# Cross-attention and FFN on one core: when the rows of later groups are normalized and turned, and which engine forms the weight sums of the first group

## Chip, core and metric

The kernel runs on one core of a Trainium2 chip. The metric is the device time of one execution in microseconds. In the profile PE is TensorE (PEld its weight loads), DVE is VectorE, ACT is ScalarE, POOL is GpSimd and SP is SyncE, which issues nearly all the DMAs.

## What is computed

Sixteen sequences of 128 tokens with 1024 features go through one block: cross-attention on a context of the same shape, and a linear layer with fixed 0/1 weights. All is float32.

```python
x = x + xattn(layernorm(x), ctx, ctx, Wq, bq, Wk, bk, Wv, bv, Wo, bo)   # 32 query heads, 8 key heads of 32
x = x + scale * (concat(n[:819], -4 * n[819:]) @ kernel)                # n = layernorm(x), kernel 1024x1024 of 0/1
```

Wq and Wo are 1024x1024, Wk and Wv 1024x256. In attention each key head serves four query heads; the softmax runs over 128 keys.

## The kernel before, in words

**Groups and stages.** The 16 sequences (batches b) are worked in eight groups of two. Each group passes: context transposed, keys (`prep_k`) and values (`prep_v`); x normalized and transposed, queries (`prep_q`); four *attends*, one for each batch and each half a of the heads, in the order (b0, a0), (b1, a0), (b0, a1), (b1, a1); the output product (`out_proj`); the second norm and the FFN (`ffn`). The stages of neighbouring groups overlap: while group g's four attends run, PE also does the output product of g-1, keys, values and queries of g+1 and the FFN of g-1. In the first group that filler is the rest of its own queries and the keys, values and queries of group 1.

**Order of the work.** The order on each engine is written out by the program: `Stream` holds a queue of generators that emit pieces of PE work with a planned duration, and events put in with `later(us, fn)` that are emitted when the planned clock has passed. Planned times only choose the order; on the chip each engine works through its own queue in order and waits for semaphores. So an instruction that waits holds up all that stands behind it on its engine.

**An attend.** `scores` (L559) makes four score tiles; for each, DVE takes the maximum (negm, L571), ACT four exponentials (L575), DVE a reciprocal and a product (inv, p, L586 and L587), PE turns p (tpp, L592), ACT copies it (pt, L594); `weighted` (L602) multiplies with the values.

**Products by seven.** Queries of group 1 on and all output products use a seven-product scheme for 2x2 blocks (`seven`, L453). It needs sums of weight blocks: `combine` (L767) forms them once, in the first group, on DVE (L781: four steps of two 128x512 operations each for Wq's halves k = 0 and 1 and for Wo's halves 0 and 1), and SP stores them to DRAM (L784). Weight pieces of 512 KB are read into a ring of eight buffers (`fetch`, L219), each when PE has used up an earlier one. The queries of the first group alone are made plainly (`prep_q_plain`, L413, eight outputs; ACT writes batch 0's and DVE batch 1's, L430 and L433).

**Norms and transposes.** `norm_x` (L381) normalizes rows in place: two statistics, an aggregate and an addition on DVE, the reciprocal root on GpSimd (L285), the scaling on DVE (L286). The rows of groups 0 and 1 are then transposed by PE (`turned`, L334). From group 2 on, `turn_x` (L348) normalizes, has SP store the rows to DRAM and load them back by 32-row blocks (`through_dram`, L296), and DVE turns the blocks (L361). The context is turned by DVE (`turn_ctx`, L343). Rows x, blocks turn_x and turn_f share two buffers of the tag "turn".

**Where the change touches.** `get_x` (L859) loads x of a group and plans its `turn_x`; both are called, with `prep_ctx`, at the start of the group before the one they serve, beside the output product (L916, L917). In the first group L898 to L913 give the order; `sums_of_wo` (L847) and `sums_of_wq` (L875) spread the weight sums. `load_by_quadrants` (L160) loads Wk and Wv in four DMAs each, `through_dram` of the second norm is timed by `FBACK` (L814) and `late` (L683).

Of the kernel before, what the change touches and what calls it, by code (L numbers as in the profile page):

```python
# [17 lines left out]
P = 128  # L18
# [58 lines left out]
def once(fn, *args):  # L77
    fn(*args)
    yield 0.0
# [3 lines left out]
def kernel(  # L83
# [74 lines left out]
        cs[b] = c_t  # L158

    def load_by_quadrants(dst, w, queues):  # L160
        src = w.rearrange("(k c f) n -> k f c n", k=NB, f=32)
        for k in range(NB):
            queues[k % len(queues)].dma_start(out=dst[k * 32 : (k + 1) * 32], in_=src[k])

    def load_x(b, tag="row"):

# [178 lines left out]
            src[:, :, h * HC : (h + 1) * HC],  # L345
        )

    def turn_x(b, store, back, turn):  # L348

        grp, j = b // GB, b % GB  # L350
        src = xns.pop(b)
        stats = new_stats(f"a{b}")
        for k in range(D // HALF):
            half_stats(stats, src, k)
        row = work.tile([P, D], FP, tag="row", name=f"xq{b}", bufs=2)
        normalize(by_quadrant(row), by_chunk(src), stats, f"a{b}")

        def blocks(c_t, h=0):
            if (grp, h) not in xTs:
                xTs[grp, h] = work.tile([P, HC, T], FP, tag="tT", name=f"xT{grp}_{h}", bufs=TB)  # L360
            nc.vector.transpose(  # L361
                xTs[grp, h][:, :, j * S : (j + 1) * S].rearrange("p c (t n) -> p t c n", t=NB),
                c_t[:, :, h * HC : (h + 1) * HC],
            )
            if h == 0:
                stream.later(1.5, lambda: blocks(c_t, 1))

        through_dram(row, f"x{b}", store, back, turn, blocks)

    def prep_ctx(grp, *us):  # L370

        for n, at in enumerate(us):
            stream.later(at, lambda n=n: turn_ctx(grp * GB + n % GB, n // GB))

    def prep_x(grp, h):
# [37 lines left out]
    def prep_q_plain(a, at):  # L413

        for j in range(GB):
            qTs[j, a] = work.tile(S4, FP, tag="qT", name=f"qT{j}_{a}", bufs=6)
        for g in range(NG):
            mm = ps_mm.tile([P, GB, S], FP, tag="mm", name=f"q_{a}_{g}")
            k, cols = g // 2, slice(g % 2 * P, (g % 2 + 1) * P)
            yield from accumulate(  # L420
                mm,
                [
                    (
                        pieces[at[c // HC, k]].rearrange("p (c n) -> p c n", c=HC)[:, c % HC, cols],
                        chunk(xTs, 0, c),
                    )
                    for c in range(NC)
                ],
            )
            nc.scalar.activation(  # L430
                qTs[0, a][:, g], mm[:, 0], AF.Identity, bias=bqs[:, a, g : g + 1], scale=scale
            )
            nc.vector.tensor_scalar(  # L433
                qTs[1, a][:, g], mm[:, 1], scale, bqs[:, a, g : g + 1], MULT, ADD
            )
            yield 0.85

    def product(mm, pairs, start):
# [175 lines left out]
    def out_proj(grp):  # L614
# [12 lines left out]
        def run():  # L627
            b0 = grp * GB
            half = {f"a{j + 1}{a + 1}": yTs.pop((b0 + j, a)) for j in range(GB) for a in range(NA)}
            s = {n: work.tile(S4, FP, tag="comb", name=f"s{n}_{grp}", bufs=4) for n in range(1, 5)}  # L630

            def sum_(n, left, right, op):
                left = s[left] if left in s else half[left]
                right = s[right] if right in s else half[right]
                nc.vector.tensor_tensor(s[n], left, right, op)
# [12 lines left out]
            def product_of(prod, mm, start):  # L648
                lhsT = half[prod.split()[0]]
                for k in range(2):  # L650
                    w = pieces[ids[prod, k]].rearrange("p (c n) -> p c n", c=2)
                    for c in range(2):
                        nc.tensor.matmul(  # L653
                            mm,
                            lhsT=lhsT[:, 2 * k + c],
                            rhs=w[:, c],
                            start=start and k == c == 0,
                            stop=k == c == 1,
                            skip_group_check=True,
                        )  # L660
                    fetch()
                    yield 2 * HALF / 600

            def read(mm, c):
                j, h = int(c[1]) - 1, int(c[2]) - 1
                x_t, cols = xs[b0 + j], slice(h * HALF, (h + 1) * HALF)
                nc.vector.tensor_add(x_t[:, cols], mm, x_t[:, cols])  # L667
                reads[c] += 1
                if reads[c] < (1 if c == "c21" else 2):
                    return  # L670
                stream.later(1.0, lambda: half_stats(stats[j], x_t, h) and None)
                if c in ("c12", "c21"):
                    def norm():
                        b = b0 + j
                        x2n = work.tile([P, D], FP, tag="row", name=f"x2n{b}", bufs=2)
                        if b < B - 2 * GB:
                            normalize(by_quadrant(x2n), by_chunk(x_t), stats[j], f"f{b}")
                            through_dram(x2n, f"f{b}", 3.0, *FBACK[j], lambda t: split_blocks(b, t))
                        else:
                            normalize(x2n, x_t, stats[j], f"f{b}")  # L680
                            x2ns[b] = x2n

                    late = 0.0 if b0 + j >= B - 2 * GB else 4.0  # L683
                    stream.later(late + (3.0 if c == "c12" else 4.5), norm)

            yield from seven(f"o{grp}", product_of, read)
# [77 lines left out]
            stream.later(0.7 + 2.4 * i, first)  # L764
        return pts

    def combine(w, k, part):  # L767

        if w == "q":

# [7 lines left out]
        for dst, left, right, op in ops:  # L778
            for h in range(2):
                cols = slice(h * HALF, (h + 1) * HALF)  # L780
                nc.vector.tensor_tensor(dst[:, cols], left[:, cols], right[:, cols], op)  # L781
            yield
        for n, t in enumerate(order):
            nc.sync.dma_start(out=sums[w, n + 1, k], in_=t)  # L784
# [16 lines left out]
    def load_o_part(k):  # L801
# [7 lines left out]
                part[r, o] = t  # L809
        return part  # L810

    BLOCKS = [(r, o) for r in range(2) for o in range(2)]
    NGRP = B // GB
    FBACK = ((12.0, 22.0), (14.0, 26.0))  # L814
    with tc.manual_schedule():
        stream = Stream()

# [27 lines left out]
            norm_x(j)  # L845

        def sums_of_wo():  # L847
            def then():
                o_parts.append(load_o_part(1))
                for j in range(GB):  # L850
                    load_x(GB + j, "turn")
                load_ffn()

            stream.later(4.0, lambda: spread(combine("o", 0, o_parts[0]), 1.5, then))

        stream.add(prep_x(0, 0), prep_x(0, 1), once(sums_of_wo), plain(0))
        stream.run(0.0, lambda: stream.queue)

        def get_x(grp):  # L859

            for j in range(GB):
# [29 lines left out]
        for grp in range(NGRP):  # L891
# [121 lines left out]
```

## Time and profile before

| | |
|---|---|
| median of 3 runs | 805.54 us (805.47 to 806.14) |
| the profiled execution | 805.76 us |
| its span, first to last instruction | 804.0 us |
| PE busy | 773.9 us (96%) |
| DVE busy | 489.1 us (61%) |
| ACT busy | 321.4 us (40%) |
| POOL busy | 71.0 us (9%) |
| mean granted PE clock | 0.996 |
| moved by DMA | 190.31 MB |

A row of a timeline gives start, length, engine, line, operation, what is written and read, and in brackets the idle time before it with the one who ended it. A row of waits gives engine and line, who was waited for, total us, times, and the longest. Matmuls of 128x128 weights start every 0.11, 0.22 or 0.43 us for 128, 256 or 512 columns when nothing holds them; the lengths shown are longer, since they overlap.

### The profile page before, as it was taken

The page shows a single profiled execution, that of the slowest core. Times are in us where ns is not written, and L with a number is a line of the kernel's source. Part 1 is how long each engine was busy: PE and PEld are TensorE (multiplying, and loading weights), DVE is VectorE, ACT ScalarE, POOL GpSimd, SP SyncE. Part 2 cuts the span into 40 slices and gives each one's busy share as a digit, 9 for nine tenths or more (in the row PEclk, how much of TensorE's full clock was granted, in tenths as well). Part 3 has the DMA queues.
Part 4 walks back from the last instruction along what each step waited for, and adds up shares of the span by engine and source line. Part 5 has one row for each costly group of instructions (what it writes and reads, how often), then busy time and mean ns, then how long its engine had stood idle before and what let it go on. Part 6 is the DMA issues. An engine that isn't in the chain of part 4 may idle for free.

```text
span 804.0 us, 13722 instructions
## 1 busy us (share of the span) xinstructions
PE 773.9 (96%) x5024; PEld 574.4 (71%) x5024; DVE 489.1 (61%) x910; ACT 321.4 (40%) x1257; POOL 71.0 (9%) x109
## 2 busy tenths in 40 slices
PE   3998999999999999999999999999999999999998
PEld 3886795589846897479864798548984689646556
DVE  1369756756487564866647575675647856567442
ACT  0143674344334352344433444334434445466100
POOL 1000003010010201001010100102001010100300
PEclk9999899999999999999999999999999999999999
DMA  9999499888488983889659984689847867562511
GB/s 204 360 312 319 155 372 393 265 252 270 143 283 271 249 263 140 305 252 283 208 188 293 271 264 156 244 263 261 263 158 270 293 198 260 181 214 74 197 45 79
DMA packets 98355, 190.31 MB, mean 237 GB/s; under 512 B 7888, under 2 KB 57040, under 8 KB 98288
## 3 DMA queue, kind: packets, MB, share of 16 engines
q1 hardware_dynamic: 96480, 187.73, 72.4%
q10 hardware_dynamic: 1664, 1.57, 1.1%
q8 instruction: 40, 0.66, 0.3%
q0 software_dynamic: 144, 0.14, 0.1%
q14 instruction: 27, 0.22, 0.1%
HBM read 160.04 MB, written 29.36 MB: 236 GB/s over the span
## 4 chain that ended last, share of the span: by engine, by line
PE 76%; DVE 12%; DMA 6%; issue 3%; SPq 1%; POOL 1%; ACT 0%; ACTq 0%; POOLq 0%; DVEq 0%
PE f L317 15%; PE q_u L442 13%; PE o_u L653 9%; PE q_v L442 6%; PE v L317 6%; PE tpp L592 6%; PE k L317 5%; PE o_v L653 5%; PE sc L559 4%; PE av L602 4%; PE q_c L442 3%; DVE p L587 2%; DVE st_a L277 2%; DVE x L667 2%; DVE cT L343 2%
## 5 line engine op out<-in xcount | busy, mean ns | idle before, releaser
L575 ACT ACTIVATE p<-sc,negm 128x128 f32<-128x128 f32 x512 | 181.0, 368 | 152.8 <-DVE negm L571 91.6
L594 ACT COPY pt<-tpp 128x512 f32<-128x512 f32 x128 | 74.6, 589 | 139.7 <-PE tpp L592 139.2
L571 DVE TENSOR_REDUCE negm<-sc 128x4 f32<-128x512 f32 x128 | 86.9, 681 | 38.2 <-PE sc L559 37.5
L317 PE MATMUL f<-wf_sb,x2l 128*128 128x512 f32 x256 | 105.4, 412 | 0.0
L575 ACT ACTIVATION_READ_ACCUMULATOR p<-sc,negm 128x1 f32 x512 | 105.2, 205 | 0.0
L317 PE MATMUL f<-wf_sb,x2h 128*128 128x512 f32 x256 | 101.1, 395 | 0.0
L587 DVE TENSOR_TENSOR p<-p,inv 128x512 f32<-128x512 f32 x128 | 89.8, 701 | 4.4
L179 POOL TENSOR_TENSOR x<-x,bo_b 128x256 f32<-128x256 f32 x64 | 50.2, 815 | 376.4 <-DMA x<-in_x_dram 318.5
L592 PE MATMUL tpp<-ident,p 128*128 128x128 f32 x512 | 76.8, 275 | 6.1 <-DVE p L587 4.0
L592 PEld LDWEIGHTS tpp<-ident,p 128*128 128x128 f32 x512 | 62.6, 142 | 27.6 <-issue 18.1
L442 PE MATMUL q_u<-t,piece 128*128 128x128 f32 x672 | 80.9, 275 | 0.0
L442 PEld LDWEIGHTS q_u<-t,piece 128*128 128x128 f32 x672 | 77.9, 192 | 0.0
L317 PE MATMUL v<-wv_sb,cT 128*128 128x256 f32 x256 | 63.0, 397 | 12.1 <-DMA wv_sb<-in_L_xattn_Wv_dram 12.1
L737 DVE SCALAR_TENSOR_TENSOR x<-f,fscale,x 128x512 f32<-128x512 f32 x32 | 24.0, 750 | 75.0 <-PE f L317 74.9
L653 PE MATMUL o_v<-piece,s 128*128 128x512 f32 x128 | 60.8, 601 | 2.9 <-DVE x L667 2.9
L653 PE MATMUL o_u<-piece,s 128*128 128x512 f32 x128 | 59.6, 598 | 3.4 <-DVE x L667 3.4
L317 PEld LDWEIGHTS v<-wv_sb,cT 128*128 128x128 f32 x256 | 49.6, 201 | 18.6 <-issue 12.1
L653 PE MATMUL o_u<-piece,yT 128*128 128x512 f32 x128 | 58.5, 599 | 0.0
L317 PE MATMUL k<-cT,wk_sb 128*128 128x256 f32 x256 | 57.8, 379 | 0.0
L317 PEld LDWEIGHTS f<-wf_sb,x2l 128*128 128x128 f32 x256 | 48.2, 188 | 10.9 <-issue 1.1
L317 PEld LDWEIGHTS f<-wf_sb,x2h 128*128 128x128 f32 x256 | 48.2, 188 | 10.3 <-issue 0.5
L317 PEld LDWEIGHTS k<-cT,wk_sb 128*128 128x128 f32 x256 | 48.0, 190 | 8.9 <-issue 2.6
(82 smaller groups left out, 911.9 us busy)
## 6 DMA issues: line engine op xcount, KB each, us to landing
piece<-o SPq DMA_DIRECT2D x64, 512.0 KB, 4.4
piece<-q SPq DMA_DIRECT2D x56, 512.0 KB, 5.9
piece<-in_L_xattn_Wq_dram SPq DMA_DIRECT2D x50, 512.0 KB, 5.8
piece<-in_L_xattn_Wo_dram SPq DMA_DIRECT2D x48, 512.0 KB, 4.5
xn<-in_x_dram SPq DMA_DIRECT2D x16, 512.0 KB, 5.4
x<-in_x_dram SPq DMA_DIRECT2D x16, 512.0 KB, 4.9
ctx<-in_ctx_dram SPq DMA_DIRECT2D x60, 128.0 KB, 7.3
out_dram<-x SPq DMA_DIRECT2D x15, 512.0 KB, 3.0
```

The source lines that it names most:

```text
L179: lambda cut=cut: nc.gpsimd.tensor_add(x_t[:, cut], x_t[:, cut], bo_b[:, cut]) and None,
L317: nc.tensor.matmul(mm, lhsT=lhsT, rhs=rhs, start=k == 0, stop=k == n - 1)
L442: nc.tensor.matmul(mm if part is None else mm[:, part], lhsT=lhsT, rhs=rhs, start=start and n == k == 0, stop=k == len(some) - 1, skip_gro ...
L559: nc.tensor.matmul(tiles[i][:, g], lhsT=qT[rows, g], rhs=kT[rows, a, cols], start=True, stop=True,)
L571: nc.vector.tensor_reduce(negm, tile_, AX.X, ALU.max, negate=True)
L575: nc.scalar.activation(p[:, g], tile_[:, g], AF.Exp, bias=negm[:, g : g + 1], accum_out=total[:, g : g + 1],)
L587: nc.vector.tensor_mul(p, p, inv.unsqueeze(2).to_broadcast([P, NG, S]))
L592: nc.tensor.transpose(tp[:, g], p[:, g], ident)
L594: nc.scalar.copy(pt, tp)
L602: nc.tensor.matmul(mm[i * HD : (i + 1) * HD], lhsT=vs[b][:, h * HD : (h + 1) * HD], rhs=pts[i], start=True, stop=True,)
L653: nc.tensor.matmul(mm, lhsT=lhsT[:, 2 * k + c], rhs=w[:, c], start=start and k == c == 0, stop=k == c == 1, skip_group_check=True,)
L737: nc.vector.scalar_tensor_tensor(x_t[:, cut], mm, fscale, x_t[:, cut], ALU.mult, ALU.add)
```

## The change

1. Rows of x for groups 2 to 7 are loaded, normalized and sent through DRAM (`get_x`, `rows_x`) one group earlier, beside the FFN (for group 2: beside the queries of group 1); the contexts are turned there too. The turning of the rows stays in the following group (`turn_rows`), at planned 30 to 36 us. The second norm is planned 4 us later, its way through DRAM shorter (`late`, `FBACK`).
2. `combine` takes an engine; Wo's sums and Wq's for k = 1 go to GpSimd, Wq's for k = 0 stay on DVE.
3. In the first group ACT writes the queries of both batches for a = 0.
4. Rows of group 1 are normalized inside the second plain product (after its 7th and 13th piece of work) and not after Wq's sums; they and the FFN weights are loaded before the second part of Wo, not after.
5. Wk and Wv are loaded in halves of four chunks: eight DMAs each, not four.

```diff
     def load_by_quadrants(dst, w, queues):
         src = w.rearrange("(k c f) n -> k f c n", k=NB, f=32)
-        for k in range(NB):
-            queues[k % len(queues)].dma_start(out=dst[k * 32 : (k + 1) * 32], in_=src[k])
+        for h in range(2):
+            cut = slice(h * NC // 2, (h + 1) * NC // 2)
+            for k in range(NB):
+                queues[k % len(queues)].dma_start(
+                    out=dst[k * 32 : (k + 1) * 32, cut], in_=src[k][:, cut]
+                )
...
-    def turn_x(b, store, back, turn):
-        grp, j = b // GB, b % GB
+    rows = {}
+    def rows_x(b):
         src = xns.pop(b)
...
         normalize(by_quadrant(row), by_chunk(src), stats, f"a{b}")
...
-            if h == 0:
-                stream.later(1.5, lambda: blocks(c_t, 1))
-        through_dram(row, f"x{b}", store, back, turn, blocks)
+        through_dram(row, f"x{b}", 2.5, 7.0, 7.0, lambda c_t: rows.update({b: c_t}))
+    def turn_x(b, h):
+        grp, j = b // GB, b % GB
...
+        c_t = rows.pop(b) if h == 1 else rows[b]
+        nc.vector.transpose(
+            xTs[grp, h][:, :, j * S : (j + 1) * S].rearrange("p c (t n) -> p t c n", t=NB),
+            c_t[:, :, h * HC : (h + 1) * HC],
+        )
...
-            nc.scalar.activation(
-                qTs[0, a][:, g], mm[:, 0], AF.Identity, bias=bqs[:, a, g : g + 1], scale=scale
-            )
-            nc.vector.tensor_scalar(
-                qTs[1, a][:, g], mm[:, 1], scale, bqs[:, a, g : g + 1], MULT, ADD
-            )
+            for j in range(GB):
+                if j == 0 or a == 0:
+                    nc.scalar.activation(
+                        qTs[j, a][:, g], mm[:, j], AF.Identity, bias=bqs[:, a, g : g + 1], scale=scale
+                    )
+                else:
+                    nc.vector.tensor_scalar(
+                        qTs[j, a][:, g], mm[:, j], scale, bqs[:, a, g : g + 1], MULT, ADD
+                    )
...
-                    late = 0.0 if b0 + j >= B - 2 * GB else 4.0
+                    late = 0.0 if b0 + j >= B - 2 * GB else 8.0
...
-    def combine(w, k, part):
+    def combine(w, k, part, engine=nc.gpsimd):
...
-                nc.vector.tensor_tensor(dst[:, cols], left[:, cols], right[:, cols], op)
+                engine.tensor_tensor(dst[:, cols], left[:, cols], right[:, cols], op)
...
-    FBACK = ((12.0, 22.0), (14.0, 26.0))
+    FBACK = ((7.0, 22.0), (8.0, 24.0))
...
         def sums_of_wo():
-            def then():
-                o_parts.append(load_o_part(1))
+            def inputs():
                 for j in range(GB):
                     load_x(GB + j, "turn")
                 load_ffn()
-            stream.later(4.0, lambda: spread(combine("o", 0, o_parts[0]), 1.5, then))
+            def then():
+                o_parts.append(load_o_part(1))
+            stream.later(10.0, inputs)
+            stream.later(8.0, lambda: spread(combine("o", 0, o_parts[0]), 3.3, then))
...
-                stream.later(10.0 + 3.0 * j, lambda b=b, j=j: turn_x(b, 3.5, 7.0 + j, 16.0 + 2.0 * j))
+                stream.later(5.0 + 4.0 * j, lambda b=b: rows_x(b))
+        def turn_rows(grp):
+            for n, at in enumerate((30.0, 32.0, 34.0, 36.0)):
+                stream.later(at, lambda n=n: turn_x(grp * GB + n // 2, n % 2))
...
-                    spread(combine("o", 1, o_parts[1]), 2.5)
-            spread(combine("q", k, {(r, o): pieces[at_q[r, o, k]] for r, o in BLOCKS}), 1.5, then)
+                    spread(combine("o", 1, o_parts[1]), 3.3)
+            part = {(r, o): pieces[at_q[r, o, k]] for r, o in BLOCKS}
+            if k == 0:
+                spread(combine("q", k, part, nc.vector), 1.5, then)
+            else:
+                spread(combine("q", k, part), 3.3, then)
...
                     once(prep_ctx, nxt, 12.5, 13.5),
-                    between(plain(1), 9, sums_of_wq, 0),
+                    between(
+                        between(between(plain(1), 7, norm_x, nxt * GB), 9, sums_of_wq, 0),
+                        13,
+                        norm_x,
+                        nxt * GB + 1,
+                    ),
                     once(sums_of_wq, 1),
                     once(turn_ctx, nxt * GB, 1),
                     once(turn_ctx, nxt * GB + 1, 1),
-                    once(norm_x, nxt * GB),
                     prep_k(nxt),
                     once(get_ctx, nxt + 1),
-                    once(norm_x, nxt * GB + 1),
                     prep_v(nxt),
                     prep_x(nxt, 0),
                     prep_x(nxt, 1),
+                    once(get_x, nxt + 1),
+                    once(prep_ctx, nxt + 1, 14.0, 18.0, 22.0, 26.0),
                     once(convert_ffn),
                     between(qs[nxt], 40, residuals, grp),
...
-                    once(get_x, nxt),
-                    once(prep_ctx, nxt, 3.7, 8.0, 13.0, 18.0),
+                    once(turn_rows, nxt),
                     os[grp - 1],
                     once(get_ctx, nxt + 1),
                     prep_k(nxt),
                     once(load_residual, b0, 4.0),
                     prep_v(nxt),
                     qs[nxt],
+                    once(get_x, nxt + 1),
+                    once(prep_ctx, nxt + 1, 2.5, 7.0, 11.0, 16.0),
                     ffn(p0),
                     once(load_residual, b1, 2.0),
```

More of the change, by code (lines that the diff above doesn't have):

```diff
@@ L356, in turn_x @@
         normalize(by_quadrant(row), by_chunk(src), stats, f"a{b}")
[L358 to L363, printed above, removed]
-            )
-            if h == 0:
-                stream.later(1.5, lambda: blocks(c_t, 1))
-        through_dram(row, f"x{b}", store, back, turn, blocks)
+        through_dram(row, f"x{b}", 2.5, 7.0, 7.0, lambda c_t: rows.update({b: c_t}))
+    def turn_x(b, h):
+        grp, j = b // GB, b % GB
+        if (grp, h) not in xTs:
+            xTs[grp, h] = work.tile([P, HC, T], FP, tag="tT", name=f"xT{grp}_{h}", bufs=TB)
+        c_t = rows.pop(b) if h == 1 else rows[b]
[3 more added lines that the diff above has]
+        )
     def prep_ctx(grp, *us):
-        for n, at in enumerate(us):
+        for n, at in enumerate(us if grp < NGRP else ()):
             stream.later(at, lambda n=n: turn_ctx(grp * GB + n % GB, n // GB))
@@ L429, in prep_q_plain @@
             )
-            nc.scalar.activation(
-                qTs[0, a][:, g], mm[:, 0], AF.Identity, bias=bqs[:, a, g : g + 1], scale=scale
-            )
-            nc.vector.tensor_scalar(
-                qTs[1, a][:, g], mm[:, 1], scale, bqs[:, a, g : g + 1], MULT, ADD
-            )
+            for j in range(GB):
[7 more added lines that the diff above has]
+                    )
             yield 0.85
@@ L810, in load_o_part @@
         return part
+    NGRP = B // GB
     BLOCKS = [(r, o) for r in range(2) for o in range(2)]
-    NGRP = B // GB
-    FBACK = ((12.0, 22.0), (14.0, 26.0))
+    FBACK = ((7.0, 22.0), (8.0, 24.0))
     with tc.manual_schedule():
@@ L859, in get_x @@
         def get_x(grp):
-            for j in range(GB):
+            for j in range(GB if grp < NGRP else 0):
                 b = grp * GB + j
                 load_x(b, "turn")
-                stream.later(10.0 + 3.0 * j, lambda b=b, j=j: turn_x(b, 3.5, 7.0 + j, 16.0 + 2.0 * j))
+                stream.later(5.0 + 4.0 * j, lambda b=b: rows_x(b))
+        def turn_rows(grp):
+            for n, at in enumerate((30.0, 32.0, 34.0, 36.0)):
+                stream.later(at, lambda n=n: turn_x(grp * GB + n // 2, n % 2))
         def get_ctx(grp):
```

## The prediction, made before the changed kernel ran

> **What bounds the kernel now.** The page's slices come first. TensorE (PE) is busy in 96% of a span of 804.0 us, so only PE's gaps can be won:
>
> ```profile
> PE   3998999999999999999999999999999999999998
> PEclk9999899999999999999999999999999999999999
> ```
>
> Apart from the start they lie in slices 3 to 5 (60 to 100 us), with a clock below full in the fifth. PE's waits, asked for 10 to 128 us and then for one later group (318.79 to 414.56 us), name the releasers (total us, times, longest):
>
> ```profile
> PE tpp L592 <- DVE p L587: 4.0, 2, 3.4
> PE q L317 <- DVE qT L433: 1.0, 1, 1.0
> PE tpp L592 <- ACT p L575: 0.8, 1, 0.8
> ```
>
> ```profile
> PE o_u L653 <- DVE x L667: 0.7, 1, 0.7
> PE o_v L653 <- DVE x L667: 0.6, 1, 0.6
> ```
>
> Nearly all are VectorE (DVE) being late. Windows around the longest gap (length, PE, PEld, DVE, ACT, POOL busy, granted clock, DMA):
>
> ```profile
> 77.24:80.66 3.42, 1.25 (x6) 0.76 (x4) 2.69 (x6) 0.38 (x1) 0.78 (x3) 1.00 1.08 280
> 80.66:84.07 3.41, 2.21 (x8) 1.98 (x9) 2.86 (x8) 2.56 (x10) 0.00 (x0) 0.50 1.02 410
> 84.07:87.48 3.41, 3.41 (x12) 2.77 (x11) 1.77 (x3) 0.18 (x1) 0.00 (x0) 0.50 0.28 112
> ```
>
> One stretch with PE 1.25 of 3.42 us busy is followed by 6.83 us at half clock; PE resumes at 81.86, so (87.48 - 81.86) / 2 = 2.8 us are lost on top of the gap.
>
> I call the first group's four attends A1 to A4, S the start of the second plain query product on PE (46.51), U the end of A3's scores (90.30), G the first output product (127.33). By the order of the two programs PE's instructions are the same, one for one; DVE, ACT, POOL and SP move against them. The sum is made against the profiled execution's own 805.76 us (span 804.0 plus 1.8), 0.2 above the median of 805.54.
>
> **Groups 1 to 6: -8.1.** In a group PE should go from o_v (331.72, four at 0.43) on at 333.44 and goes on at 334.25; after tpp (338.23, 0.44 long) it should go on at 338.67 and does at 339.43: 0.81 + 0.76 = 1.57. Four such groups, 1.44 in group 1, 0.4 in group 6: 8.1. There the change takes off DVE four context transposes (0.61 apart) and two norms of x (3.07 each with the reciprocal root on POOL): 8.6 us of a stretch 318.8 to 341 in which DVE never rests. The wait goes whole; next late would be a score tile, which DVE takes at once. The norms go beside the FFN, where DVE stood idle 2.87, 3.86 and 2.98 us before three reads of f; the tightest place is the second read, at about 406.8 after a norm waiting for its row (landing about 402.3), while PE wants the buffer at 408.1. Bounds -8.3 (the restarts too) to -6.5 (0.3 given back in five groups); the rows sit near the first. SP's stores and loads for x leave a stage with DMA share 0.9 for one with 0.5 and wait there behind nothing PE needs: the ring of eight weight pieces is full.
>
> **Before S: -1.3, start 0.** ScalarE writes both queries of the first product and DVE no longer stands before a late Wo part, so the 0.28 at 40.7 and 1.04 at 46.5 go (PE q waits above). ScalarE's four extra writes (0.37 each) end 0.8 after a product, buffers are wanted 3.4 after. Halved weights are eight DMA issues more, of 0.46 each on SP's and ScalarE's queues, which wait for landings there anyway; they let v begin some 3 us before 12.1, but x's rows land near 20.7 as before (same bytes, same order), so the norm chain sets the transposes: 0.9 earlier at most. PE then rests about 2 us before them, and half clock for one 3.4 us window would cost 1.7. I take 0, bounds -1.3 to +1.5.
>
> **S to U: +2.6.** Now 43.8 us, of which 0.92 + 0.76 + 3.52 gap and 2.8 clock; clean 35.8. In the new order DVE has both norms of x2 and x3 ahead of the context transposes that k needs. DVE's queue by its own rows (maximum 0.6, reciprocal and p 0.8, read of q 0.26, pair of sums 1.25, transpose 0.61, norm 3.07), in us after S, where the read of q comes at 4.2 as before: maximum, p1 5.9; maximum, wait for exponentials, p2 7.6; norm of x2 10.6; read, maximum, p3 12.3; pair 13.5; read after ScalarE's 14.3; p4 15.2; pair 16.4; norm of x3 19.5; two transposes 20.7; pair, read, pair 23.5; two transposes 24.7. PE wants p3 and p4 some 0.9 earlier in all, the first transposes at 18.7 (2.0 late) and the second at 22.5 (2.2 late; before they ended at 65.88 = S+19.4, just in time). A2's softmax, clear of sums and norms, then keeps up. 35.8 + 0.9 + 2.0 + 2.2 = 40.9: -2.9.
>
> Against it stands POOL. Its sums are 128x512; no row shows that. The 256-wide one takes 0.695 alone (2.78/4): 0.70 if all were fixed, 1.39 if nothing; 1.25 as an estimate by DVE's ratio (0.42 to 0.69, 0.15 fixed). While POOL works, a two-input DVE operation is slow (start, us):
>
> ```profile
> 125.83 5.72 POOL L179 TENSOR_TENSOR x<-x,bo_b 128x256 f32<-128x256 f32 x7 [0.63 <-DMA x<-in_x_dram]
> ```
>
> ```profile
> 128.02 1.13 DVE L635 TENSOR_TENSOR s<-yT,yT 128x512 f32<-128x512 f32 x1
> 129.19 1.10 DVE L635 TENSOR_TENSOR s<-s,yT 128x512 f32<-128x512 f32 x1
> ...
> 133.94 0.69 DVE L587 TENSOR_TENSOR p<-p,inv 128x512 f32<-128x512 f32 x1
> ```
>
> So 0.42 each, beside an operation half as long; twice that beside 512. POOL starts Wq's second half right after the second norm's root (about S+19), beside DVE's last four sums: 0.45 + 3 x 0.84 = 3.0. (Wo's sums beside A1's first p, 0.7, are left to the upper bound: that p is ready 1.0 before PE wants it.) PE then rests about 5.3 us inside k; as above, half clock until a full window is busy, 3.4 to 6.8 us, costs 1.7 to 3.4: 2.5. 40.9 + 3.0 + 2.5 = 46.4, that is +2.6. Bounds -2.9 (no contention, no gating) to +4.5. The Trainium skill (SBUF — State Buffer, Who interferes with whom) says that such a pair is an exclusive lock held for the whole instruction; read so, the first sum waits half a POOL operation and each other a whole one of 1.25, 4.4 in place of 3.0, and the term would be +4.0. The row agrees that they collide but shows 0.42 beside a pitch of 0.695.
>
> **U to G: +10.5.** Now 37.0 us with no gap. In the new order SP's loads of x4 and x5 stand behind piece<-q loads, which wait for PE to free pieces:
>
> ```profile
> 94.60 6.12 SPq L219 DMA_DIRECT2D piece<-q  x5
> ```
>
> The third of the five waits for half of q_c (98.14); the loads of x follow the fourth, at 98.9 = U+8.6. DVE reaches x4's statistics at U+8.0, right after A3's second p, and behind them in its queue stand A3's fourth maximum and third p, for which PE waits here:
>
> ```profile
> 102.87 0.60 PE L592 MATMUL tpp<-ident,p 128*128 128x128 f32 x4
> ```
>
> Landings: fastest piece 4.2, slowest x row 9.3, the piece issued just ahead at 98.6 took 6.7. I take 6.9: U+15.5. Norm 3.07, maximum 0.6, reciprocal 0.2, p 0.7, and 0.5 for Wo's second sums then on POOL: U+20.5 instead of the 12.57 PE wants: 8.0. Clock after such a rest 2.5. Bounds: 4.9 + 1.7 = 6.6 to 10.1 + 3.4 = 13.5. Nothing covers it: this stage is all PE. The second norm and the stores of Wo's sums come when PE is 10 us later and fit.
>
> **Sum.** 0 - 1.3 + 2.6 + 10.5 - 8.1 = +3.7: 809.5 us. All lower ends: -1.3 - 1.3 - 2.9 + 6.6 - 8.3 = -7.2, 798.6; all upper ends: +1.5 - 1.3 + 4.5 + 13.5 - 6.5 = +11.7, 817.5.
>
> **Rivals.**
> 1. Not slower: A3's wait is short. If the load of x4 lands in 4 to 5 us and the clock is hardly gated, U to G costs 5.5 to 6.6 and the sum is 804.5 to 805.6; with POOL not holding DVE (-2.9) 799.0 to 800.1. It decides from a cost of 6.8 there on: below it the sum turns negative. For it: the DMA share drops to 0.2 in places between 97 and 105. Against it: SP's order and DVE's order are fixed, and 4.2 is the fastest row. Chance 0.31.
> 2. GpSimd becomes the bound: 1.39 us per sum, each DVE operation waiting nearly as long; Wo's sums then hold back the first norm's root too. S to U +4.5, U to G 10.5 to 13.5: 811.4 to 814.4, and 817 with the groups' lower gain. For it the rows 1.13 and 1.10; against it POOL is free from 53 to 65. Chance 0.10.
> 3. It doesn't do what it says: the gaps in the output products stay, because the reads of x wait for something other than DVE's norms: 817.6. Against it: DVE's row before the late read is the norm's, and it has no idle there. Chance 0.04.
> 4. The forecast, 806 to 814: 0.55.
>
> **How the numbers follow.** A measurement of this kernel can tell about 0.2% (1.6 us) from no change. Faster than 804.1 needs most of rival 1 with its second half: 0.22. Between: 0.15, the rest of rival 1 and the edge of the forecast. Slower 0.63. The range that leaves out 2 in 10 is 800.5 to 816.0; the forecast's own stands above.
>
> **What would show it.** Right: no PE wait for DVE x L667 in groups 1 to 5, period near 94.2; a PE wait of tpp for DVE p of 6 to 9 us some 12 us after A3's scores, DVE idle at that time on DMA x; PE waiting in k for cT; half clock twice. Wrong: x4 landing before DVE wants it; DVE sums at 0.69 beside POOL's; a new PE wait in the FFN on DVE x L737, which would eat the groups' gain.

## The result, and the profile after

| | before | changed |
|---|---|---|
| median | 805.84 us (805.47 to 806.4) | 810.41 us (809.15 to 811.68) |
| ratio to before, 95% interval | | 1.0056 [1.0039, 1.0074] |
| the profiled execution | 805.76 us | 811.68 us |
| its span | 804.0 us | 809.9 us |
| mean granted PE clock | 0.996 | 0.987 |

The changed kernel is slower, by 4.6 us of medians; the forecast was 809.5. The profiled execution happens to be the slowest of its four, 5.9 above that of before. The page's slices (PE's busy tenths, and the clock) come first again:

```profile
span 809.9 us, 13739 instructions
PE   5996959999999999999999999999999999999997
PEclk9997979999999999999999999999999999999999
```

From the seventh slice to the last stage PE has no gap: from 140 to 700 us no wait of PE is listed, where before had 6.3 us in eleven waits for DVE's x. Slices 4 and 6 are new holes, each with a slow clock behind. PE's waits from 10 to 140 us (total, times, longest):

```profile
PE tpp L600 <- DVE p L595: 10.3, 3, 9.6
PE v L322 <- DMA wv_sb<-in_L_xattn_Wv_dram: 9.3, 1, 9.3
PE k L322 <- DVE cT L348: 7.3, 2, 4.5
```

The last is new, and the first is one wait of 9.6. Windows around both (length, PE, PEld, DVE, ACT, POOL busy, clock, DMA share, GB/s):

```profile
63.00:65.77 2.77, 0.00 (x1) 0.01 (x1) 2.77 (x4) 0.00 (x0) 2.77 (x3) 1.00 0.75 297
66.16:69.57 3.41, 3.00 (x8) 1.81 (x6) 3.41 (x4) 0.00 (x0) 3.41 (x3) 0.51 0.00 0
69.57:73.67 4.10, 0.00 (x0) 0.00 (x0) 4.10 (x5) 0.00 (x0) 4.10 (x4) 0.92 0.75 301
73.67:79.81 6.14, 6.14 (x15) 4.88 (x16) 3.07 (x7) 3.82 (x20) 4.20 (x5) 0.50 1.02 321
105.58:115.16 9.58, 0.00 (x2) 0.03 (x1) 5.17 (x9) 1.12 (x7) 4.14 (x4) 0.76 0.93 370
115.16:120.77 5.61, 5.61 (x27) 5.61 (x28) 4.84 (x9) 4.28 (x8) 3.35 (x4) 0.50 0.41 128
```

In the first and third PE stands still and DVE and POOL are busy all the time; in the fifth DVE rests for part. After each, PE works at half clock. VectorE's queue around the fifth (start, length):

```profile
100.35 0.69 DVE L595 TENSOR_TENSOR p<-p,inv 128x512 f32<-128x512 f32 x1
109.22 1.29 DVE L282 BATCH_NORM_STATS2 st_a<-xn 128x6 f32<-128x512 f32 x2 [8.18 <-DMA xn<-in_x_dram]
...
111.60 1.74 DVE L291 TENSOR_SCALAR xq<-xn,mv_a,rs_a 128x1024 f32<-128x1024 f32 x1 [0.67 <-POOL rs_a L290]
113.27 0.68 DVE L579 TENSOR_REDUCE negm<-sc 128x4 f32<-128x512 f32 x1
...
114.06 0.95 DVE L595 TENSOR_TENSOR p<-p,inv 128x512 f32<-128x512 f32 x1
```

DVE stood 8.18 us at x4's statistics with A3's maximum and p ready to run behind them.

Where the time went, by the marks of the prediction (S, U, G), in us of the profiled executions. The kernels below the changed one are the experiments.

| kernel | ratio to before [95%] | start to S | S to U | U to G | G to end |
|---|---|---|---|---|---|
| before | | 46.5 | 43.8 | 37.0 | 676.7 |
| changed | 1.0056 [1.0039, 1.0074] | 43.3 | 49.6 | 48.9 | 668.2 |
| e1_stats_later | 0.9991 [0.9979, 1.0002] | 43.1 | 48.3 | 38.3 | 671.5 |
| e2_norms_back | 0.9992 [0.9983, 1.0002] | 43.5 | 40.5 | 49.5 | 669.6 |
| e3_sums_vector | 0.9971 [0.9958, 0.9984] | 43.0 | 41.8 | 48.0 | 667.4 |
| e4_weights_whole | 1.0094 [1.0078, 1.0109] | 44.7 | 48.7 | 48.5 | 667.9 |
| e5_loads_ahead | 0.9973 [0.9959, 0.9987] | 43.1 | 48.5 | 39.2 | 669.6 |
| e6_later_groups_only | 0.9897 [0.9877, 0.9917] | 46.7 | 42.7 | 37.0 | 669.1 |
| f1_vector_later | 0.9910 [0.9889, 0.9931] | 43.1 | 41.8 | 38.3 | 673.9 |
| f2_vector_ahead | 0.9857 [0.9836, 0.9878] | 43.2 | 41.8 | 38.0 | 668.6 |
| g1_second_norm_back | 0.9880 [0.9850, 0.9909] | 42.7 | 38.7 | 40.8 | 668.8 |
| g2_queries_split | 0.9872 [0.9849, 0.9896] | 42.7 | 41.8 | 38.0 | 671.6 |
| g3_norm_last | 0.9872 [0.9852, 0.9892] | 43.0 | 38.7 | 38.4 | 672.0 |
| g4_wo_gpsimd | 0.9874 [0.9851, 0.9896] | 43.0 | 38.3 | 40.5 | 669.1 |

### The profile page after: what moved, and what is told of

It is laid out like the page before. It is cut to its first block, busy times and chain, and to the rows that moved or that the text cites. A ratio compares the mean times of both kernels' runs of the same rounds, so it can differ in the third digit from the quotient of the medians.

```text
span 809.9 us, 13739 instructions
## 1 busy us (share of the span) xinstructions
PE 776.4 (96%) x5024; PEld 578.6 (71%) x5024; DVE 489.9 (60%) x882; ACT 322.5 (40%) x1261; POOL 109.2 (13%) x133
## 4 chain that ended last, share of the span: by engine, by line
PE 85%; DMA 5%; issue 5%; POOL 2%; SPq 2%; DVE 1%; ACT 0%; ACTq 0%; POOLq 0%
PE f L322 15%; PE o_u L661 14%; PE q_u L450 12%; PE o_v L661 7%; PE tpp L600 7%; PE q_v L450 6%; PE v L322 5%; PE k L322 5%; PE sc L567 4%; PE av L610 4%; PE o_c L661 3%; PE q_c L450 3%; DMA wo<-in_L_xattn_Wo_dram 2%; POOL wo L789 1%; SPq L224 1%
## 5 line engine op out<-in xcount | busy, mean ns | idle before, releaser
L184 POOL TENSOR_TENSOR x<-x,bo_b 128x256 f32<-128x256 f32 x64 | 54.3, 875 | 145.2 <-DMA x<-in_x_dram 145.2
L322 PE MATMUL k<-cT,wk_sb 128*128 128x256 f32 x256 | 62.5, 401 | 7.3 <-DVE cT L348 7.3
L322 PEld LDWEIGHTS k<-cT,wk_sb 128*128 128x128 f32 x256 | 50.8, 201 | 18.1 <-DVE cT L348 8.2
L567 PEld LDWEIGHTS sc<-kT,qT 32*128 32x128 f32 x1024 | 31.4, 186 | 25.7 <-issue 25.7
```

What stands on the lines that cost most here:

```text
L184: lambda cut=cut: nc.gpsimd.tensor_add(x_t[:, cut], x_t[:, cut], bo_b[:, cut]) and None,
L322: nc.tensor.matmul(mm, lhsT=lhsT, rhs=rhs, start=k == 0, stop=k == n - 1)
L567: nc.tensor.matmul(tiles[i][:, g], lhsT=qT[rows, g], rhs=kT[rows, a, cols], start=True, stop=True,)
```

## The experiments

Every kernel is compared with before on its own chip, where before took 804.4 to 805.5 in the median and not 805.84; so ratios weigh more than the times against which the expectations were written. Edits are against the changed kernel unless another is named.

**e1: the norms of x4 and x5 later.**

```diff
-                stream.later(5.0 + 4.0 * j, lambda b=b: rows_x(b))
+                at = 14.0 if grp == 2 else 5.0
+                stream.later(at + 4.0 * j, lambda b=b: rows_x(b))
```

> Only the planned time of the two norms of x4 and x5 (group 2's rows) is later, by 9 us, so that on VectorE A3's fourth maximum and its third and fourth p stand ahead of x4's statistics; loads, sums and norms of the other groups are the changed kernel's. Theory: TensorE's 9.6 us wait for A3's third p is VectorE standing in its queue at statistics whose rows have not landed. Then the wait goes whole, the clock stays full there, U to G falls from 48.9 to 37 to 38 us, and the time from 810.4 to 798.5 (797 to 801). Rival: the stage is late anyway (GpSimd's second Wo sums, or x4's rows now too late for group 1): the wait moves to A4's p or to group 1's first products, U to G stays above 42 or group 1 grows by as much, and the time is 804 or more.

Measured 803.95 us. The wait for p and the slow clock behind it are gone, U to G is 38.3: VectorE's queue was the cause. But of 10.6 us won there 3.4 came back in group 1, as the rival said, since SyncE now takes the rows' loads through DRAM (129.62 to 134.97) just before most pieces of Wo's sums (135.49 on). So the time lies above the range of the theory. PE's waits from 85 to 150 us:

```profile
PE o_u L661 <- DMA piece<-o: 3.3, 2, 2.1
PE tpp L600 <- ACT p L583: 1.1, 1, 1.1
```

**e2: the norms of x2 and x3 behind the context transposes, as before.**

```diff
-                    between(between(between(plain(1), 7, norm_x, nxt * GB), 9, sums_of_wq, 0),
-                        13, norm_x, nxt * GB + 1),
+                    between(plain(1), 9, sums_of_wq, 0),
...
+                    once(norm_x, nxt * GB),
                     prep_k(nxt),
                     once(get_ctx, nxt + 1),
+                    once(norm_x, nxt * GB + 1),
```

> Undoes the first half of item 4: the norms of x2 and x3 stand on VectorE behind the context transposes again, as in the kernel before; all else is the changed kernel. Theory: the 2.8 and 4.5 us that TensorE waits in k for cT come from the norms ahead of the transposes (3.1 each, the second 4.0 beside GpSimd). Then the first wait goes whole, the second falls to at most 2.5 (the four sums beside GpSimd's stay slow), S to U falls from 49.6 to 38 to 42, and the time from 810.4 to 800 to 804. Rival 1, collisions with GpSimd's sums are the cause: the second wait stays above 3.5, S to U at 45 or more. Rival 2, it only moves: A2's softmax is late as in the kernel before (tpp for p 3 to 5 us), S to U 43 to 45, time 804 to 807.

Measured 804.04 us; both waits in k are gone, S to U is 40.5. Part moved, as rival 2 had it: the three waits for p total 13.5 with a longest of 10.7, so 2.8 us stand in A2 (with 3.41 us at half clock behind them), and 1.5 in a wait for a piece of Wo in group 1. S to U is within the theory's range, the time just above it.

**e3: all sums on VectorE.**

```diff
-    def combine(w, k, part, engine=nc.gpsimd):
+    def combine(w, k, part, engine=nc.vector):
```

> Undoes item 2 alone: all sums on VectorE again, at the planned times of the changed kernel; GpSimd has only roots and residuals in the first group. Theory: beside GpSimd's sums each two-input operation of VectorE takes 1.6 to 1.75 us where it takes 0.65 alone, and this is 4 us of the second wait in k. Then the DVE sums are back at 0.65, the second wait in k falls from 4.5 to 1 or less, the first from 2.8 to 1.5 to 2.5, but Wo's and half of Wq's sums (16 us in 24 operations) now stand ahead of p's on VectorE: S to U 44 to 47, U to G about as now (48 to 51); time 806 to 811. Rival: only the order of the norms counts: both waits in k stay within 1 us of theirs, S to U 49 to 51, time 810 to 813.

Measured 802.0 us, better than either side expected; S to U is 41.8. VectorE with GpSimd's sums beside it, in the changed kernel:

```profile
62.76 1.74 DVE L291 TENSOR_SCALAR xn<-xn,mv_a,rs_a 128x1024 f32<-128x1024 f32 x1 [0.67 <-POOL rs_a L290]
64.42 1.29 DVE L348 STREAM_TRANSPOSE cT<-ctx 128x512 f32<-128x512 f32 x2
65.64 3.43 DVE L789 TENSOR_TENSOR piece<-piece,piece 128x512 f32<-128x512 f32 x2
...
69.25 3.15 DVE L789 TENSOR_TENSOR piece<-piece,piece 128x512 f32<-128x512 f32 x2
72.33 1.29 DVE L348 STREAM_TRANSPOSE cT<-ctx 128x512 f32<-128x512 f32 x2
```

And the same instructions in e3, GpSimd at rest:

```profile
62.75 0.82 DVE L291 TENSOR_SCALAR xn<-xn,mv_a,rs_a 128x1024 f32<-128x1024 f32 x1 [0.66 <-POOL row_w L260]
63.49 1.29 DVE L348 STREAM_TRANSPOSE cT<-ctx 128x512 f32<-128x512 f32 x2
64.70 1.25 DVE L789 TENSOR_TENSOR piece<-piece,piece 128x512 f32<-128x512 f32 x2
...
66.14 1.28 DVE L789 TENSOR_TENSOR piece<-piece,piece 128x512 f32<-128x512 f32 x2
67.33 1.29 DVE L348 STREAM_TRANSPOSE cT<-ctx 128x512 f32<-128x512 f32 x2
```

Four sums take 6.6 us and not 2.5, the scaling 1.74 and not 0.82, the transposes the same. The second transposes start at 67.33 and not 72.33; PE's waits in k fall from 7.3 to 3.7 and neither drew half clock. The 24 sums of some 0.63 us that came back to VectorE cost next to nothing (a wait for q grew from 0.4 to 0.7): it had room for them in rests beside v (four sums at once, 79.65 to 82.1).

**e4: Wk and Wv whole.**

```diff
-        for h in range(2):
-            cut = slice(h * NC // 2, (h + 1) * NC // 2)
-            for k in range(NB):
-                queues[k % len(queues)].dma_start(
-                    out=dst[k * 32 : (k + 1) * 32, cut], in_=src[k][:, cut]
-                )
+        for k in range(NB):
+            queues[k % len(queues)].dma_start(out=dst[k * 32 : (k + 1) * 32], in_=src[k])
```

> Undoes item 5 alone: Wk and Wv in four DMAs each. Theory: the first transposes start 1.8 us earlier in the changed kernel (26.0 against 27.8) because v begins 2.8 earlier on half of Wv; then this kernel starts them near 27.8 and takes 812.2 (811.5 to 813). Rival: the start is earlier by the landing of that one execution: they start within 0.5 of 26.0 and the time is 810.4.

Measured 811.87 us; v starts at 11.8 and the first transposes at 27.5, where the changed kernel has 9.3 and 26.0. The halves gain, as the theory said: 1.5 by the start of the transposes, 0.38% by the two ratios, whose intervals do not overlap.

**e5: x4's and x5's loads ahead of four fetches.**

```diff
         def sums_of_wq(k):
             def then():
-                for _ in range(4):
-                    fetch()
-                if k == 1:
+                if k == 0:
+                    four()
+                else:
                     spread(combine("o", 1, o_parts[1]), 3.3)
...
                     once(get_x, nxt + 1),
+                    once(four),
```

Here `four` makes the four fetches.

> Only SyncE's order differs from the changed kernel: the loads of x4 and x5 stand ahead of the four fetches of weight sums that follow Wq's second combine, not behind them; VectorE's queue is the changed kernel's, statistics of x4 ahead of A3's third p. Theory: x4's load waits at SyncE behind fetches that wait for TensorE to free pieces. Then the loads issue when TensorE has turned x2 and x3, about U+2.5 and not U+8.7, x4 lands 4.5 to 7 later at U+7 to U+9.5, VectorE hardly waits, p follows 5.8 after the landing, and TensorE's 9.6 us wait falls to 0 to 3 without half clock: U to G 37 to 41, time from 810.4 to 799 to 803.5. Rival: the landing is set by the traffic, not by the issue: x4 lands after U+13, the wait is 6 or more, U to G 45 or more, time 807 or more.

Measured 803.05 us, U to G 39.2. SyncE in the changed kernel, then in e5:

```profile
97.15 4.37 SPq L224 DMA_DIRECT2D piece<-q  x4
101.57 0.90 SPq L173 DMA_DIRECT2D xn<-in_x_dram  x2
```

```profile
93.57 0.82 SPq L173 DMA_DIRECT2D xn<-in_x_dram  x2
95.84 7.60 SPq L224 DMA_DIRECT2D piece<-q  x8
```

The loads issue at U+2.0 instead of U+8.7 and land in 3.5 to 4.4 us instead of 7.6 to 8.4, with no four pieces issued just ahead. VectorE takes the statistics with no rest, and the wait of 9.6 is 1.3. So the wait had two conditions, and repairing either one removes it, or nearly: the place of the load on SyncE, and the place of the statistics on VectorE.

**e6: before with item 1 alone**, for the rows of groups 3 to 7; the first group's instructions are those of before, and `get_x_old` does group 2's rows as before. Against the changed kernel, beside items 2 to 5 undone:

```diff
+                    *((once(get_x_old, nxt), once(prep_ctx, nxt, 3.7, 8.0, 13.0, 18.0))
+                        if grp == 1 else (once(turn_rows, nxt),)),
-                    once(turn_rows, nxt),
...
-                    once(get_x, nxt + 1),
-                    once(prep_ctx, nxt + 1, 14.0, 18.0, 22.0, 26.0),
                     once(convert_ffn),
```

> The kernel before with item 1 alone, from the rows of group 3 on: the first group's instructions are those of before on every engine, group 2's rows are prepared in group 1 as before, rows of groups 3 to 7 one group earlier, with the later second norm. Theory: item 1's gain is the 1.57 us of gaps in each later group's output product and owes nothing to the first group; group 1's 1.4 stays. Then first output product to end is 676.7 less 6.5 to 7, and the time is 6.5 (5.5 to 7.2) below the kernel before, 0.991 to 0.993 of it. Rival: the gain needs the changed first group (rows, pieces or Wo's sums further ahead): less than 3 of it comes, or new waits of 2 or more stand in group 1 or 2.

Measured 797.32 us, 0.9897. Of the gaps in the output products only group 1's are left:

```profile
PE o_u L657 <- DVE x L671: 0.6, 1, 0.6
PE o_v L657 <- DVE x L671: 0.5, 1, 0.5
```

G to end is 7.6 below before, 0.6 more than expected. With S to U 1.1 shorter, by a shorter stretch at half clock (3.41 us and not 6.83), the median is 8.2 below before, outside the expected 5.5 to 7.2. Item 1's gain is its own, and stands without items 2 to 5.

**f1: e3 and e1 together.**

```diff
+    def combine(w, k, part, engine=nc.vector):
...
+                at = 14.0 if grp == 2 else 5.0
```

> Two edits of the changed kernel together: all sums on VectorE, and the norms of x4 and x5 planned 9 us later. Theory: the two costs are separate. All sums on VectorE gives S to U 41 to 43 (49.6 in the changed kernel), the later norms U to G 37 to 39 (48.9), and up to 3.3 come back in group 1 where the pieces of Wo's sums stand behind the rows' way through DRAM: 791.5 to 796. Rival: Wo's second sums on VectorE and the later norms meet in A4: TensorE waits there for p 3 us or more and the time is 797 to 801.

Measured 798.6 us, above the range and within that of the rival, whose reason did not come: A4 has no wait for p but one of 1.07 for ScalarE. S to U and U to G came as expected; what came back in group 1 is more than the 3.3: a wait of 3.05 for a piece, and 6.7 us at half clock behind it.

```profile
133.46 6.74 PE L661 MATMUL o_u<-piece,s 128*128 128x512 f32 x8 [3.05 <-DMA piece<-o]
140.04 1.88 PE L661 MATMUL o_v<-piece,s 128*128 128x512 f32 x4
```

Eight matmuls of 512 columns take 6.74 us here; the next four, at full clock, 1.88.

**f2: e3 and e5 together, the norms of x4 and x5 4 us later.**

```diff
+    def combine(w, k, part, engine=nc.vector):
...
+                at = 9.0 if grp == 2 else 5.0
...
+                    once(four),
```

> All sums on VectorE, the loads of x4 and x5 ahead of the four fetches on SyncE, and their norms planned 4 us later (not 9). Theory: with x4 landed when VectorE comes to it, the place of its norm costs A3 nothing or little, and the rows' way through DRAM is over before SyncE has to fetch the pieces of Wo's sums: S to U 41 to 43, U to G 37 to 40, first output product to end 667 to 669: 790 to 794. Rival: as the later norms alone, group 1 waits for pieces 3 us: 794 to 797.

Measured 794.07 us (793.42 to 795.03), 0.9857 of before: the lowest ratio of all, 1.4% below before, though the intervals of g1 to g4 overlap with its own. Its page has no slice below full clock and no hole behind the first:

```profile
PE   5998999999999999999999999999999999999998
PEclk9999999999999999999999999999999999999999
```

**g1: f2 with the norm of x3 behind the context transposes**, inside v.

```diff
-                        between(between(plain(1), 7, norm_x, nxt * GB), 9, sums_of_wq, 0),
-                        13, norm_x, nxt * GB + 1,
+                        between(plain(1), 7, norm_x, nxt * GB), 9, sums_of_wq, 0,
...
-                    prep_v(nxt),
+                    between(prep_v(nxt), 6, norm_x, nxt * GB + 1),
```

> The kernel with all sums on VectorE, x4's and x5's loads ahead of the four fetches and their norms 4 us later (794.07), with one edit more: the norm of x3 stands behind the context transposes, inside the product for v, not ahead of them. Theory: the two waits of 1.8 and 1.9 us in k that are left are the 3.1 us of that norm ahead of cT. Then both go (0.5 at most left), S to U falls from 41.8 to 38 to 38.7, A2's p keep up, and the time is 790 to 791.5. Rival: VectorE has no room for the norm beside A2's p and Wq's second sums: TensorE waits 1.5 us or more for p or for x3's rows after U, and the time is 792.5 or more.

Measured 795.03 us (792.77 to 797.28), above the range. The waits in k went nearly as expected (0.7 left, S to U 38.7), and the gain was given back at the third query product, which waits for a piece of Wq's second sums. They come through DRAM, and the last of them now stands behind that norm; g3 tests whether this is the reason. PE's row there:

```profile
93.97 1.01 PE L450 MATMUL q_u<-t,piece 128*128 128x128 f32 x4 [2.50 <-DMA piece<-q]
```

**g2: f2 with item 3 undone.**

```diff
-                if j == 0 or a == 0:
+                if j == 0:
```

> The same base (794.07) with item 3 undone: VectorE writes batch 1's queries of the first product again, as in the kernel before, with Wo's sums on VectorE planned later than there. Theory: the 1.3 us of waits before S in the kernel before came from Wo's sums standing ahead of reads while their rows had not landed; planned 4 us later they stand behind most reads, so item 3 itself is worth nothing here: first transposes to S within 0.4 of 17.9 and the time within 1 of 794.1. Rival: ScalarE's writing is what removed them: they return, S is 0.8 to 1.5 later and the time 795 to 796.

Measured 794.69 us; S at 42.7 against f2's 43.2, and from the first transposes to S 17.9 us in both. Once Wo's sums are planned later, item 3 shows no worth; the intervals would hide 1 us either way. G to end is 3.0 longer than in f2, with waits of 1.9 for a piece of Wo and 1.8 for VectorE's x; no run tells whether that is the edit or this execution, the slowest of its four.

**g3: g1 with that norm behind the last sums.**

```diff
-                    between(prep_v(nxt), 6, norm_x, nxt * GB + 1),
+                    between(prep_v(nxt), 7, norm_x, nxt * GB + 1),
```

> As the kernel whose norm of x3 stands behind the context transposes (795.03), but the norm stands one piece of TensorE's work later, behind the last of Wq's second sums, not ahead of them. Theory: what that kernel gave back, 2.5 us of wait for a piece of Wq's sums at the third query product and 3.4 us at half clock after it, is those last sums 3.1 us later, their store and their load. Then the wait is 0 to 0.5 and the clock full, U to G 38.0 to 38.5, S to U 38.5 to 39, and the time 788.5 to 791. Rival: the pieces are late because TensorE is 3.4 us earlier with the same chain of sums, store and load: a wait of 1.5 or more stays, 792 to 794.

Measured 793.95 us (0.9872, no different from f2). U to G is 38.4 as expected, but 1.7 of the wait for a piece stays, as the rival said, and two more waits for pieces follow. PE's waits from 80 to 150 us:

```profile
PE o_c L661 <- DMA piece<-in_L_xattn_Wo_dram: 2.4, 1, 2.4
PE o_u L661 <- DMA piece<-o: 1.7, 1, 1.7
PE q_u L450 <- DMA piece<-q: 1.7, 1, 1.7
```

These three, the longest, are transfers: a first group that is 3 us quicker meets SyncE's chain of stores and fetches. For VectorE PE still waits 0.7 each at q, tpp and k.

**g4: g3 with Wo's sums on GpSimd**, Wq's on VectorE.

```diff
-    def combine(w, k, part, engine=nc.vector):
+    def combine(w, k, part, engine=nc.gpsimd):
...
-                spread(combine("q", k, part), 3.3, then)
+                spread(combine("q", k, part, nc.vector), 3.3, then)
```

> The same kernel with Wo's sums alone on GpSimd (16 operations), Wq's all on VectorE. Theory: sums on GpSimd cost where VectorE has operations of two inputs ahead of something TensorE waits for (Wq's sums ahead of cT in the changed kernel), not as such: beside Wo's sums stand A1's and A3's p and group 1's t, with slack of about 1 us, and the time is within -1.5 and +2 of its partner. Rival: every collision reaches TensorE: p and t twice as long give 4 us or more, and waits for p of 1 us or more appear in A1 and A3.

Measured 794.28 us, within 0.4 of g3. The collisions do reach PE once, 2.2 us for a read of q behind two slowed t's, with half clock after it. PE therefore comes to the output product 1.7 us later (G at 121.81 and not 120.09), while SyncE fetches Wo's pieces at nearly the same times as in g3 (from 110.47 and from 110.39); so g3's waits of 2.4 and 1.7 for pieces fall away, and one of 1.3 for VectorE stands there (G to end 669.1 against 672.0). The collision cost nothing here because PE would otherwise have waited for transfers; that GpSimd's sums cost nothing as such is not shown. In the changed kernel they stood where VectorE had to bring cT, and nothing hid them.

## Why the prediction was right, and where its steps were off

Direction and time came out: +3.7 forecast, +4.6 by the medians, +5.9 in the profiled execution. Of the five terms three left their own bounds, in both directions, so the nearness of the total is in part luck: against the profiled execution the start and the groups came 1.8 and 0.4 lower than forecast, S to U and U to G 3.2 and 1.4 higher.

**Start: 0 forecast (-1.3 to +1.5), -1.8 measured.** The step that failed: x's rows "land near 20.7 as before", so that the norm chain sets the transposes, "0.9 earlier at most". VectorE took x's statistics at 19.79, right behind the addition for v, so the rows were there, and PE went from k into the transposes without a rest, in both kernels. The product for v set it, and e4 shows that the halves gave its earlier start. The half clock that I feared after a rest did not come, since there was no rest. But v began 2.8 earlier and the transposes only 1.8, since v itself took longer (before, then changed):

```profile
12.11 8.97 PE L317 MATMUL v<-wv_sb,cT 128*128 128x256 f32 x32 [12.11 <-DMA wv_sb<-in_L_xattn_Wv_dram]
9.30 9.96 PE L322 MATMUL v<-wv_sb,cT 128*128 128x256 f32 x32 [9.30 <-DMA wv_sb<-in_L_xattn_Wv_dram]
```

In the changed kernel's first 3.4 us of v only eight matmuls run, 0.42 each where 0.22 is the full pace, though the profile lists the clock as full there. How long that lasts differs between executions: e1, e3 and e5, with the same loads, have the transposes at 25.1 to 25.2 and not 26.0.

**Before S: -1.3 forecast, -1.4 measured**, with a reason too many. Both ScalarE's writing and the moved sums were credited; e3 (sums on VectorE) has S at 43.0 and g2 (queries on VectorE) at 42.7, so planning Wo's sums later is enough. In e6, with before's first group, Wo's rows reach VectorE's sums at nearly the same times as in before (43.85 and 43.70), but the transposes start 1.6 us later, and from them to S it takes 17.3 us as in the changed kernel (18.7 in before). So the wait depends on whether PE comes before Wo's rows.

**S to U: +2.6 forecast (-2.9 to +4.5), +5.8 measured.** The waits in k were 2.77 + 4.52 = 7.3; the forecast had 2.0 + 2.2 for the order and 3.0 for the collisions, 7.2. By e3 the order alone costs 3.7, and the collisions add 3.6. The term mis-sized is the clock: I counted one rest, 2.5 with an end at 3.4. There are two rests with a half-clock stretch each, in which PE was busy for 3.0 and 6.14 us: half of 9.1 is 4.6. Not all of that is lost time, for a slow stretch ahead of a wait shortens the wait: in e5, with the same order and the same collisions, the first rest drew no half clock, PE came sooner and waited 5.9 in the second, not 4.5, and S to U is only 1.1 shorter. The rest is small: 1.1 in three waits of A1 where 0.9 stood, and restarts. The price of a collision was low as well: 0.84 for each sum by the ratio to a 256-wide one, and 4.05 for four by the rows above; and the norm's scaling, which I had not seen as colliding, takes 0.92 more. e2 and e3 show that the two causes don't add: without either one S to U is 40.5 or 41.8, and without the collisions and with x3's norm moved back (g1) 38.7.

The rows on collisions stand beside the Trainium skill (SBUF — State Buffer, Who interferes with whom): operations of VectorE with two inputs in SBUF, and those in a two-port mode, which tensor_scalar can enter, contend with GpSimd; with at most one input in SBUF and outside those modes they do not. The rows agree: sums (1.65 for 0.63) and the scaling (1.74 for 0.82) are slowed, transposes (1.29 a pair) and maxima (0.68) are not. Read as a lock held for the whole instruction it had made the four sums 4.4 longer; 4.05 was measured.

**U to G: +10.5 forecast (6.6 to 13.5), +11.9 measured.** Step by step, in us after U: loads issued 8.6 forecast, 8.7 measured; statistics begun 15.5 and 16.4 (7.6 from issue and not 6.9); p written 20.5 and 22.2 (the scaling 1.74, p 0.95, both beside GpSimd); p wanted 12.57 and 12.73. So the wait is 9.6 and not 8.0, and the clock 5.61 / 2 = 2.8 for 2.5. e1 and e5 confirm both halves of the reason.

**Groups 1 to 6: -8.1 forecast (-8.3 to -6.5), -8.5 measured.** The period is 94.0 (from 328.88 to 422.88, scores to scores), 94.2 was forecast; no wait for DVE in the FFN appeared. e6 has nearly all of it alone (-7.6).

**Rivals.** The first (a short wait in A3) fell with the 9.6. The third (the gaps stay) fell. The second (GpSimd becomes the bound) fell as an account of the whole, since e1, e2 and e5 each bring the time back with GpSimd untouched; its price for a collision, nearly 1.39, was high as my 0.84 was low, for the four sums took 1.01 longer each. Its upper end was added up wrongly: 814.4 with -6.5 for -8.1 in the groups is 816.0, not 817. "Half clock twice" was three times.

## What to carry to other kernels

On an engine that works its queue in order, an operation put early is not work moved into spare time but a wait put in front of everything behind it: look up when its data can land, and what stands ahead of its load on the queue that issues it. In this kernel, moving sums to GpSimd freed VectorE only where it had no sum, product or scaling of rows to do that somebody waited for. A change of many parts is worth taking apart, since here one of them (e6) carried the gain and the others together spent more than that.

## What the runs showed of the hardware

- **GpSimd's sums.** A 128x512 sum takes 1.25 us alone (two in 2.49) and 1.51 beside VectorE's (eight in 12.07); VectorE's own goes from 0.63 to about 1.65 beside them (four in 6.58).
- **The clock.** Stretches at half clock were 3.41, 6.83 or 10.24 us long, and in each profile they begin and end on a grid of 3.41 us (in the changed kernel at 66.2, 69.6, 73.0, 79.8, 110.6 and 120.8). The length of a wait alone does not decide. Waits of 1.8 and 1.9 us 3.8 apart (e3, f2), or of 2.4 and 1.7 (g3), drew none; waits of 2.2 (g4), 2.5 (g1) and 2.77 (the changed kernel) drew 3.41, of 3.05 (f1) and 4.5 drew 6.83 (f1, the changed kernel), of 9.6 drew 10.24; yet in e5 a wait of 2.77 in the same place drew none. What tells them apart, without an exception here, is how long PE was busy within one step of the grid. From 20 to 150 us, in the eleven profiles that have such stretches, every step at full clock with PE busy for 1.39 us or less was followed by one at half clock, and none with 1.55 or more was; a step at half clock was followed by full clock when PE was busy in it for 2.96 or more, and not at 2.77 or less. Examples:

| kernel | step, us | PE busy in it | clock of the next step |
|---|---|---|---|
| changed | 62.79 to 66.20 | 0.64 | 0.50 |
| e5 | 60.54 to 63.95 | 2.08 | 1.00 |
| e5 | 63.95 to 67.37 | 1.98 | 1.00 |

The changed kernel's 2.77 lies within one step, e5's is spread over two. A rest of 2 to 3 us thus may or may not cost 1.7 us, by where it falls. That goes with the Trainium skill (TensorE: Matmul & The Clock Gate, Part 1), which has the clock set by the activity in free-running windows of about 3.4 us.
